# A four-layer graph network on one core: x of four groups ahead of the weights, a third group with x^T by TensorE, later constants, halved copies, the last norm by VectorE's statistics

## The chip, the cores and the metric

The kernel runs on one core of a Trainium2 chip. The metric is the device time of one execution in microseconds. Engine names in the profile: PE is TensorE (PEld its weight loads), DVE is VectorE, ACT is ScalarE, POOL is GpSimd, SP is SyncE, which here only issues transfers.

## The reference

x has 64 samples of 256 nodes with 128 features, adj is 256 x 256, all float32. Four layers follow one another, each with a residual and a norm over the features (here cut to the core):

```python
# layer 0: Chebyshev orders 1..3 of adj, twice the same adj: 7 weights
x = layernorm(x + sum_k(adj^k @ x @ W0[..., k]))
# layer 1
x = layernorm(x + adj @ (x @ w1) + b1)
# layer 2: A = adj + I, d = rowsum(A) ** -0.5
x = layernorm(x + (d A d) @ x @ w2.T + b2)
# layer 3: five steps of a gated graph cell, in_matrix = out_matrix = adj
def step(h):
    m = adj @ h;  av = concat([m, m])
    z = sigmoid(av @ w3.T + b3 + h @ u3.T + bu3)
    r = sigmoid(av @ w4.T + b4 + h @ u3.T + bu3)
    hv = tanh(av @ w5.T + b5 + (r * h) @ u5.T + bu5)
    return (1 - z) * h + z * hv
x = layernorm(x + step^5(x))
```

## The kernel before

The samples are taken in 32 groups of two; group g starts at sample 2g. A group's tiles are 128 partitions x 512. Every piece of work (a transfer, a few matmuls, an elementwise operation) is recorded as an operation with an engine, a cost, a lag, a rank, and the values that it reads and writes. A planner (`Plan.order`) then puts all operations in order: for each engine it takes the one that can start first by the recorded costs, among equals the one of lower place (rank plus a random part), in twelve tries of which it keeps the one that ends first by its own times. The order of each engine's instructions is thereby fixed before the kernel runs, and engines work through it strictly one after the other. An operation's cost and rank steer this order only. Up to twelve groups are under way at once, so the steady state mixes all layers.

Constants are recorded with `pre(rank, engine, cost, ...)`, `load` (by default on SP's queue) and `fetch`. They are:

- `a_nat`, the adjacency; `aT`, its transpose (TensorE `turn`, then a copy, L293); `a2T`, the transpose of its square (matmuls, then a copy, L303). The first product with x reads a2T. Short transposes of the identity (`warming`) stand between.
- `w0_raw` and from it `w0s`, `w0t` (layer 0's weights, centred over the features so that the norm needs no mean);
- `ahat`, `deg`, `dinv`, `anT` (layer 2's matrix: `degree` L354 to L358, a power on GpSimd L370, `rows` L362, a turn by TensorE, `columns` L366);
- for each matrix, five sums of its 128 x 128 blocks (`block_sums`, L383 to L387), names s_aT, s_a2T, s_anT, s_aTp;
- `wb` (w1, b1, b2, centred at L320, L321), and the gate weights: raw tiles, sums of their halves (`both`, L411, L413), and transposes of these by TensorE (w435u5T, w2u3T).

A group's product with a matrix (`propagate`) has a plain form, and a form of seven 128-column products (`seven`): GpSimd makes three differences of the input (tsq, tqq and the like, L744 to L751), TensorE does four products, then a fifth, then two more, and between them ACT and VectorE make sums from the bank in place (usq L770, wsq L773, mq L776, L780). The last two products overwrite a part of the bank that mq's sum reads, so they wait for it.

`record` opens a group: it loads x and forms x^T. A group that starts below `HEAD` is near: TensorE transposes x (`ptx`, L801), the product q with a2T is plain, and `inner` does layer 0 with plain products. Any other group is far: VectorE transposes 32 x 32 blocks of x (tx, L871), SP stores it to DRAM (dx, L874) and loads it back in another order in two transfers (xT, L879), q is by `seven`, and `inner_seven` forms four differences of xT and q on VectorE (sd, ss, se, sf, L635 to L644) and does layer 0 with fewer products. A transfer waits at the head of SP's queue for what it reads, and whatever stands behind it waits too.

The last layer's end has two forms. Six samples' worth of groups at the end (`END`) use `closing`: TensorE makes the centred sum s in a bank, `spread_of` has ACT square each 128 columns with a sum (L543: an activation and a readout for each), GpSimd raises the four sums to -1/2 (rs, L547), and VectorE multiplies (L704); then the output is stored (L939).

Of the kernel before, what the change touches and what calls it, by code (L numbers as in the profile page):

```python
# [11 lines left out]
OP = mybir.AluOpType  # L12
AX = mybir.AxisListType

P = 128
NB = 2
ACTIVE = 12
HEAD = 4
LEVEL = 7
PLAIN = 0  # L20
END = 6
# [3 lines left out]
EPS = 1e-5  # L25
# [147 lines left out]
def act_cost(elements):  # L173
    return elements / 1.2 + 165
# [3 lines left out]
def kernel(  # L178
# [30 lines left out]
    nc = tc.nc  # L209
    B, N, C = x.shape  # L210
    T = N // P
# [12 lines left out]
    plan = Plan(slots, G - LEVEL)  # L224
# [10 lines left out]
    def pre(rank, engine, cost, run, reads=(), writes=(), lag=None, joint=False, after=()):  # L235
        lag = lag or {"SP": 2300, "PE": 260, "DVE": 260, "ACT": 130, "POOL": 100}[engine]
        return plan.add(engine, cost, lag, rank, run, reads, writes, after, joint)
# [4 lines left out]
    def fetch(rank, o, src, v, queue, after=()):  # L242
        e, cost = QUEUES[queue]
        return pre(rank, queue, cost, lambda: e.dma_start(o, src), [], [v], lag=5000, joint=True, after=after)

    def load(rank, name, shape, src, keep=True, queue="SP", lag=2300):
        v = constant(name, shape) if keep else Val("w", shape, name)
        e, cost = QUEUES[queue]
        pre(rank, queue, cost, lambda: e.dma_start(v.ap, src), [], [v], lag=lag)
        return v  # L250
# [3 lines left out]
    half = const.tile([P, Q], F32, name="half")  # L254
# [20 lines left out]
    a_nat = load(-9, "a_nat", [P, T, N], adj.rearrange("(t p) m -> p t m", p=P), False)  # L275
    aT, a2T = constant("aT", [P, T, N]), constant("a2T", [P, T, N])
    p_at, p_a2, p_an = temp("p_at"), temp("p_a2"), temp("p_an")

    def turn(ps, src):
        for mt in range(T):  # L280
            for nt in range(T):
                nc.tensor.transpose(ps.ap[:, mt * N + nt * P:mt * N + (nt + 1) * P],
                                    src.ap[:, nt, mt * P:(mt + 1) * P], ident)

    def flat(v):
        return v.ap.rearrange("p t n -> p (t n)")

    def turned_early():
        turn(p_at, a_nat)
        warming(4)  # L290

    pre(-8, "PE", 8 * 110, turned_early, [a_nat], [p_at, warm])
    pre(-8, "ACT", act_cost(512), lambda: nc.scalar.copy(flat(aT), p_at.ap), [p_at], [aT])  # L293

    def square():
        for mt in range(T):
# [3 lines left out]
        warming(2)  # L300

    pre(-8, "PE", pe_cost(N, 4) + 220, square, [a_nat, aT], [p_a2, warm])
    pre(-8, "ACT", act_cost(512), lambda: nc.scalar.copy(flat(a2T), p_a2.ap), [p_a2], [a2T])  # L303


    w0_raw = load(-1, "w0_raw", [P, C, K0], w0, lag=7300)

    w0s = constant("w0s", [P, 4, C])
# [16 lines left out]
    centred = pre(-7, "DVE", 1600, lambda: centre(w0s, w0m), [w0s], [w0s, w0m])  # L325
# [15 lines left out]
    aTp = constant("aTp", [P, T, N])  # L341
# [8 lines left out]
    ahat, anT = Val("w", [P, T, N], "ahat"), constant("anT", [P, T, N])  # L350
    deg, dinv = constant("deg", [P, T]), constant("dinv", [P, T])
# [14 lines left out]
            nc.vector.tensor_scalar(anT.ap[:, mt, :], p_an.ap[:, mt * N:(mt + 1) * N], dinv.ap[:, mt:mt + 1],  # L366
                                    None, op0=OP.mult)

    pre(0.3, "DVE", 1500, degree, [a_nat], [ahat, deg])
    pre(0.3, "POOL", 700, lambda: nc.gpsimd.tensor_tensor(dinv.ap, deg.ap, half[:, :T], op=OP.pow), [deg], [dinv])  # L370
    pre(0.9, "DVE", 600, rows, [ahat, dinv, w0s], [ahat])
    pre(1.1, "PE", 4 * 110, lambda: turn(p_an, ahat), [ahat], [p_an])
    pre(0.3, "DVE", 900, columns, [p_an, dinv], [anT])


    sums_of = {}
# [1 line left out]
    def block_sums(rank, name, aTs, after=()):  # L378
        v = constant(f"s_{name}", [P, 5, P])
        a11, a12, a21, a22 = (aTs.ap[:, kt, t * P:(t + 1) * P] for t in range(T) for kt in range(T))  # L380

        def run():
            nc.vector.tensor_add(v.ap[:, 0, :], a21, a22)  # L383
            nc.vector.tensor_sub(v.ap[:, 1, :], v.ap[:, 0, :], a11)
            nc.vector.tensor_sub(v.ap[:, 2, :], a11, a21)
            nc.vector.tensor_sub(v.ap[:, 3, :], a12, v.ap[:, 1, :])
            nc.vector.tensor_scalar(v.ap[:, 4, :], a22, -1.0, None, op0=OP.mult)  # L387

        pre(rank, "DVE", 1200, run, [aTs], [v], after=after)
        sums_of[aTs] = v  # L390

    block_sums(0.6, "aT", aT)
    block_sums(0.6, "a2T", a2T)
    block_sums(0.6, "anT", anT, (centred,))
    block_sums(0.7, "aTp", aTp, (centred,))

    wb, wbm = constant("wb", [P, 3, C]), constant("wbm", [P, 3])

    made = pre(-7, "DVE", 100, lambda: nc.vector.tensor_copy(wb.ap[:, 1:3, 0], w0s.ap[:, :2, 0]), [w0s], [wb])
    fetch(0.6, wb.ap[:, 0, :], w1, wb, "SP")
    for i, b in ((1, b1), (2, b2)):
        last = fetch(0.5, wb.ap[:, i, :], bass.AP(tensor=b.tensor, offset=b.offset, ap=[[0, P], [1, C]]), wb, "POOL", (made,))
    pre(0.9, "DVE", 1100, lambda: centre(wb, wbm), [wb, w0s], [wb, wbm])
    w1c, b1c, b2c = ((wb, wb.ap[:, i, :]) for i in range(3))
    raw = {name: load(0.6, f"raw_{name}", [P, src.shape[1]], src, False, lag=9000)
           for name, src in (("w2", w2), ("w4", w4_w), ("w3", w3_w), ("w5", w5_w), ("u3", u3_w), ("u5", u5_w))}
    both = {name: Val("w", [P, C], f"both_{name}") for name in ("w4", "w3", "w5", "w34")}
    for name in ("w4", "w3", "w5"):  # L410
        pre(0.4, "DVE", 220, lambda o=both[name], i=raw[name]: nc.vector.tensor_add(  # L411
            o.ap, i.ap[:, :C], i.ap[:, C:]), [raw[name]], [both[name]])
    pre(0.4, "DVE", 220, lambda: nc.vector.tensor_sub(both["w34"].ap, both["w3"].ap, both["w4"].ap),  # L413
        [both["w3"], both["w4"]], [both["w34"]])

    less = constant("less", [P, P])
# [28 lines left out]
    def nat(v):  # L445
        return v.ap.rearrange("p (q c) -> p q c", c=C)
# [21 lines left out]
    class Group:  # L468
# [68 lines left out]
        def spread_of(self, tag, s):  # L537

            y, ve, rs = self.val("w", "y" + tag), self.val("ve", "ve" + tag), self.val("rs", "rs" + tag)

            def squares():
                for q in range(self.q):
                    nc.scalar.activation(nat(y)[:, q, :], nat(s)[:, q, :], AF.Square, scale=C ** -0.5,  # L543
                                         bias=root[:, 0:1], accum_out=ve.ap[:, q:q + 1])

            def scales():
                nc.gpsimd.tensor_tensor(rs.ap, ve.ap, half[:, :self.q], op=OP.pow)  # L547

            self.act(squares, [s], [y, ve], 390 * self.q)
            self.add("POOL", 1040, 100, scales, [ve], [rs])  # L550
            return y, rs

        def normalise_centred(self, tag, s):
# [133 lines left out]
        def closing(self, y, hT, e, behind):  # L687

            s, hc = self.val("bank", "s3"), self.val("w", "hc")
            way, out_ = self.by_tile  # L690
            self.act(lambda: nc.scalar.copy(out_(hc), way(hT)), [hT], [hc])

            def turned(v, start, stop):
                for q in range(self.q):
                    mm(s.ap[:, q * P:(q + 1) * P], v.ap[:, q * P:(q + 1) * P], less.ap, start and q == 0, stop, shared=True)

            def early():
                turned(hc, True, False)
                mm(s.ap, ident, y.ap, False, False, shared=True)

            self.pe(pe_cost(P, self.q) + pe_cost(self.width), early, [hc, y, less], [s], behind=(behind,))
            self.pe(pe_cost(P, self.q), lambda: turned(e, False, True), [e, less], [s])
            o, rs = self.spread_of("3", s)
            self.dve(lambda: nc.vector.tensor_tensor(nat(o), nat(s), rs.ap[:, :, None].to_broadcast([P, self.q, C]),  # L704
                                                     op=OP.mult), [s, rs], [o])
            return o
# [152 lines left out]

        def record(self):  # L860
            x_ = self.val("x", "x")
            plan.add("SP", 450, (6000, 9000)[self.start // NB] if self.start < HEAD else 2700, self.rank() - 1.5, lambda: nc.sync.dma_start(nat(x_), self.view(x)), [], [x_],
                     self.load_gate)

            near = self.start < HEAD
# [2 lines left out]
            else:  # L868

                turn, far, xT = self.val("w", "tx"), self.val("dram", "dx"), self.val("w", "xT")  # L870
# [13 lines left out]
            y = self.normalise_centred("0", s0)  # L884


            for tag, ats, w, bias in (("1", aT, w1c, b1c), ("2", anT, w2T, b2c)):
# [15 lines left out]
                y = self.normalise_centred(tag, self.added(tag, py, yb))  # L903
# [42 lines left out]
    for i, nb in enumerate(sizes):  # L946
        group = Group(sum(sizes[:i]), nb)
        end = group.start + nb
        done = [o for o in groups if o.start + o.nb <= end - NB * ACTIVE]
        loaded = [o for o in groups if o.start + o.nb <= end - NB * (ACTIVE + 2)]  # L950
        if done:
            group.gate = (done[-1].last,)
        if loaded:
            group.load_gate = (loaded[-1].last,)
        elif group.start >= HEAD:
            group.load_gate = (groups[i - 2].first,)
        group.record()
        groups.append(group)
# [4 lines left out]
    with tc.manual_schedule():  # L963
        for op in plan.order():
            for v in op.vals:
                if v.tile is None:
# [3 lines left out]
                    if v.shape != full:  # L970
                        n = 1
# [37 lines left out]
```

## Time and profile before

| | |
|---|---|
| median of 3 runs | 1342.21 us (1341.92 to 1343.14) |
| the profiled execution's own time | 1342.32 us |
| its span in the trace | 1340.5 us |
| mean granted TensorE clock | 0.997 |
| TensorE instructions (matmul passes) | 6915 |
| VectorE, ScalarE, GpSimd instructions | 2577, 2361, 998 |

A float32 matmul shows as two passes, each with its weight load, so the trace counts each product twice; a transpose is one pass. Busy shares are those of the span. Idle time in square brackets ahead of an instruction names what ended it. A line number is that of the kernel before; almost all matmuls are at L219, since one helper issues them, so they are told apart by their tiles (out<-weights,moving).

### The profile page before, as it was taken

The numbers are of one execution on the slowest core, as the hardware profiler recorded it, in microseconds if no ns is written. First come the engines' busy times: TensorE is split into PE (matmuls) and PEld (weight loads), VectorE is DVE, ScalarE is ACT, GpSimd is POOL, SyncE is SP. The second block draws the span as 40 slices with busy tenths as digits, with TensorE's granted clock in tenths as the row PEclk, the third lists the DMA queues.
The fourth block names the chain that finished last, engine by engine and source line by source line (L and its number), as shares of the span: only waits on it lengthen the run. The fifth ranks groups of instructions, "written<-read, shape, count | busy, mean of one in ns | idle before, by whom it ended". The sixth has DMA issues, their size and how long they took to land.

```text
span 1340.5 us, 22669 instructions
## 1 busy us (share of the span) xinstructions
PE 1325.7 (99%) x6915; PEld 931.9 (70%) x6915; DVE 1039.0 (78%) x2577; ACT 773.6 (58%) x2361; POOL 636.1 (47%) x998
## 2 busy tenths in 40 slices
PE   8999999999999999999999999999999999999997
PEld 7987666667877766777766686777676776566554
DVE  7867767897778778788888797778876778777776
ACT  4587464645666664656655565655556786444445
POOL 5788352325646543447453454545345574232212
PEclk9999999999999999999999999999999999999999
DMA  7412333433433342333442343424322233333323
GB/s 190 131 33 79 88 95 87 141 107 96 115 95 111 95 121 70 110 95 103 121 124 74 108 134 87 119 71 119 101 73 68 60 111 103 112 109 95 89 85 103
DMA packets 269305, 134.87 MB, mean 101 GB/s; under 512 B 175712, under 2 KB 240864, under 8 KB 269184
## 3 DMA queue, kind: packets, MB, share of 16 engines
q1 hardware_dynamic: 268928, 133.29, 34.6%
q8 instruction: 55, 0.90, 0.3%
q0 software_dynamic: 256, 0.13, 0.1%
q14 instruction: 66, 0.54, 0.1%
HBM read 67.31 MB, written 65.80 MB: 99 GB/s over the span
## 4 chain that ended last, share of the span: by engine, by line
PE 97%; DVE 1%; DMA 1%; issue 0%; SPq 0%; ACT 0%; POOLq 0%; POOL 0%; ACTq 0%
PE pr L219 31%; PE ph L219 21%; PE pmg L219 19%; PE py L219 11%; PE pm L219 8%; PE pz L219 4%; PE pmq L219 3%; DMA x<-in_x_dram 1%; PE s L219 1%; DVE tx L871 0%; SPq L345 0%; DVE sd L635 0%; ACT y L543 0%; POOLq L1004 0%; DVE both_w L411 0%
## 5 line engine op out<-in xcount | busy, mean ns | idle before, releaser
L219 PE MATMUL pr<-mg,w435u5T 128*128 128x512 f32 x640 | 319.7, 593 | 0.0
L744 POOL TENSOR_TENSOR tsg<-h 128x256 f32<-128x256 f32 x128 | 94.0, 735 | 281.1 <-DMA h<-dh 200.4
L850 ACT ACTIVATE r<-pr,bsum 128x512 f32<-128x512 f32 x160 | 105.2, 658 | 123.4 <-PE pr L219 114.9
L850 ACT ACTIVATE pr<-pr,bsum 128x512 f32<-128x512 f32 x160 | 105.2, 658 | 118.0 <-PE pr L219 117.7
L547 POOL TENSOR_TENSOR rs<-ve,half 128x4 f32<-128x4 f32 x99 | 101.6, 1027 | 145.8 <-ACT y L543 137.2
L543 ACT ACTIVATE y<-s,root 128x128 f32<-128x128 f32 x396 | 153.7, 392 | 28.2 <-DVE s L565 25.5
L857 DVE TENSOR_TENSOR d<-ph,hT 128x512 f32<-128x512 f32 x160 | 109.6, 685 | 72.1 <-ACT ph L850 69.2
L219 PE MATMUL ph<-mg,w435u5T 128*128 128x512 f32 x320 | 163.3, 593 | 0.0
L219 PE MATMUL ph<-rh,w435u5T 128*128 128x512 f32 x320 | 162.7, 593 | 0.0
L219 PE MATMUL pr<-hT,w2u3T 128*128 128x512 f32 x320 | 162.2, 593 | 0.0
L219 PEld LDWEIGHTS pr<-mg,w435u5T 128*128 128x128 f32 x640 | 108.8, 191 | 70.3 <-issue 57.6
L850 ACT ACTIVATE ph<-ph,bsum 128x512 f32<-128x512 f32 x160 | 105.4, 659 | 57.8 <-PE ph L219 55.5
L219 PEld LDWEIGHTS pmg<-aTp,h 128*128 128x128 f32 x512 | 90.5, 196 | 64.8 <-issue 40.5
L857 DVE TENSOR_TENSOR rh<-r,hT 128x512 f32<-128x512 f32 x160 | 109.3, 683 | 33.1 <-ACT r L850 29.5
L558 ACT ACTIVATE y<-s,rs 128x128 f32<-128x128 f32 x384 | 122.1, 394 | 5.2 <-POOL rs L547 4.8
L857 DVE TENSOR_TENSOR pr<-pr,d 128x512 f32<-128x512 f32 x157 | 108.1, 691 | 1.7 <-ACT pr L850 0.5
L857 DVE TENSOR_TENSOR hT<-hT,pr 128x512 f32<-128x512 f32 x157 | 106.1, 678 | 1.3
L219 PE MATMUL pmg<-s_aTp,tsg 128*128 128x128 f32 x768 | 106.7, 275 | 0.0
L219 PEld LDWEIGHTS ph<-rh,w435u5T 128*128 128x128 f32 x320 | 58.5, 190 | 62.7 <-issue 46.2
L219 PE MATMUL pmg<-aTp,h 128*128 128x128 f32 x512 | 98.1, 279 | 0.0
L891 POOL TENSOR_TENSOR yb<-y,wb 128x512 f32<-128x512 f32 x64 | 81.7, 1277 | 34.3 <-ACT y L558 33.0
L780 DVE TENSOR_TENSOR mg<-pmg,usg 128x256 f32<-128x256 f32 x160 | 66.6, 418 | 39.7 <-PE pmg L219 38.3
(200 smaller groups left out, 2826.4 us busy)
## 6 DMA issues: line engine op xcount, KB each, us to landing
dh<-th SPq DMA_DIRECT2D x160, 256.0 KB, 2.0
h<-dh SPq DMA_DIRECT2D x256, 128.0 KB, 2.5
x<-in_x_dram SPq DMA_DIRECT2D x32, 256.0 KB, 3.2
hT<-dh SPq DMA_DIRECT2D x128, 64.0 KB, 2.1
out_dram<-y SPq DMA_DIRECT2D x32, 256.0 KB, 2.5
dx<-tx SPq DMA_DIRECT2D x30, 256.0 KB, 2.5
xT<-dx SPq DMA_DIRECT2D x60, 128.0 KB, 2.7
dn<-tn SPq DMA_DIRECT2D x29, 256.0 KB, 2.0
```

The source lines that it names most:

```text
L219: nc.tensor.matmul(o, lhsT, rhs, start=start, stop=stop, skip_group_check=shared)
L543: nc.scalar.activation(nat(y)[:, q, :], nat(s)[:, q, :], AF.Square, scale=C ** -0.5, bias=root[:, 0:1], accum_out=ve.ap[:, q:q + 1])
L547: nc.gpsimd.tensor_tensor(rs.ap, ve.ap, half[:, :self.q], op=OP.pow)
L558: nc.scalar.mul(nat(y)[:, q, :], nat(s)[:, q, :], rs.ap[:, q:q + 1])
L744: nc.gpsimd.tensor_tensor(ts.ap[:, :2 * P].rearrange("p (x c) -> p x c", x=2), ins(h)[:, 1], ins(h)[:, :, 0], op=OP.subtract)
L780: nc.vector.tensor_tensor(o(m, slice(1, 3)), o(ps, slice(1, 3), False), both, op=OP.add)
L850: self.act(lambda: nc.scalar.activation(t.ap, ps.ap, func, bias=bias[1], scale=1.0), [ps, bias[0]], [t], act_cost(self.width) + 100)
L857: self.dve(lambda: nc.vector.tensor_tensor(out(t), way(a), way(b), op=op), [a, b], [t])
L891: nc.gpsimd.tensor_tensor(nat(yb), nat(y), bias[1][:, None, :].to_broadcast([P, self.q, C]), op=OP.add)
```

## The change

- `HEAD` goes from 4 to 6, so three groups instead of two are near: group 2 (samples 4 and 5) has x^T by TensorE, the plain q and `inner`.
- The x loads of groups 0 to 3 have no gate on an earlier group, and larger planned lags; those of groups 2 and 3 were gated by the first operation of groups 0 and 1.
- The copies of aT and a2T are made in two halves, the first on ACT and the second on VectorE.
- Layer 2's matrix, block sums of anT and aTp, w1's load, the gate weights' loads and their sums get later ranks; `degree` waits for w0s.
- The last group's norm takes its variance from VectorE's statistics (`spread_at_once`) instead of ACT's squares.

```diff
-HEAD = 4
+HEAD = 6
...
-    pre(-8, "ACT", act_cost(512), lambda: nc.scalar.copy(flat(aT), p_at.ap), [p_at], [aT])
+    def halved(v, ps):
+
+        pre(-8, "ACT", act_cost(N), lambda: nc.scalar.copy(v.ap[:, 0, :], ps.ap[:, :N]), [ps], [v], joint=True)
+        pre(-8, "DVE", 420, lambda: nc.vector.tensor_copy(v.ap[:, 1, :], ps.ap[:, N:]), [ps], [v], joint=True)
+
+    halved(aT, p_at)
...
-    pre(-8, "ACT", act_cost(512), lambda: nc.scalar.copy(flat(a2T), p_a2.ap), [p_a2], [a2T])
+    halved(a2T, p_a2)
...
-    pre(0.3, "DVE", 1500, degree, [a_nat], [ahat, deg])
-    pre(0.3, "POOL", 700, lambda: nc.gpsimd.tensor_tensor(dinv.ap, deg.ap, half[:, :T], op=OP.pow), [deg], [dinv])
-    pre(0.9, "DVE", 600, rows, [ahat, dinv, w0s], [ahat])
-    pre(1.1, "PE", 4 * 110, lambda: turn(p_an, ahat), [ahat], [p_an])
-    pre(0.3, "DVE", 900, columns, [p_an, dinv], [anT])
+    pre(2.3, "DVE", 1700, degree, [a_nat, w0s], [ahat, deg])
+    pre(2.3, "POOL", 720, lambda: nc.gpsimd.tensor_tensor(dinv.ap, deg.ap, half[:, :T], op=OP.pow), [deg], [dinv])
+    pre(2.3, "DVE", 800, rows, [ahat, dinv], [ahat])
+    pre(2.3, "PE", 4 * 110, lambda: turn(p_an, ahat), [ahat], [p_an])
+    pre(2.3, "DVE", 900, columns, [p_an, dinv], [anT])
...
-    block_sums(0.6, "anT", anT, (centred,))
-    block_sums(0.7, "aTp", aTp, (centred,))
+    block_sums(2.4, "anT", anT, (centred,))
+    block_sums(2.6, "aTp", aTp, (centred,))
...
-    fetch(0.6, wb.ap[:, 0, :], w1, wb, "SP")
+    fetch(1.9, wb.ap[:, 0, :], w1, wb, "SP")
...
-    raw = {name: load(0.6, f"raw_{name}", [P, src.shape[1]], src, False, lag=9000)
+    raw = {name: load(2.0, f"raw_{name}", [P, src.shape[1]], src, False, lag=9000)
...
-        pre(0.4, "DVE", 220, lambda o=both[name], i=raw[name]: nc.vector.tensor_add(
+        pre(2.0, "DVE", 300, lambda o=both[name], i=raw[name]: nc.vector.tensor_add(
...
-    pre(0.4, "DVE", 220, lambda: nc.vector.tensor_sub(both["w34"].ap, both["w3"].ap, both["w4"].ap),
+    pre(2.0, "DVE", 300, lambda: nc.vector.tensor_sub(both["w34"].ap, both["w3"].ap, both["w4"].ap),
...
+        def spread_at_once(self, tag, s):
+
+            st, mv, ve, rs, y = (self.val(k, n + tag) for k, n in (
+                ("st", "st"), ("mv", "mv"), ("ve", "ve"), ("rs", "rs"), ("w", "y")))
+
+            def stats():
+                for q in range(self.q):
+                    nc.vector.bn_stats(st.ap[:, q * 6:(q + 1) * 6], nat(s)[:, q, :])
+                for q in range(self.q):
+                    nc.vector.bn_aggr(mv.ap[:, 2 * q:2 * q + 2], st.ap[:, q * 6:(q + 1) * 6])
+                nc.vector.tensor_scalar(ve.ap, mv.ap.rearrange("p (q k) -> p k q", k=2)[:, 1], EPS, None, op0=OP.add)
+
+            self.dve(stats, [s], [st, mv, ve], 260 * self.q + 110)
+            self.add("POOL", 1040, 100, lambda: nc.gpsimd.tensor_tensor(rs.ap, ve.ap, half[:, :self.q], op=OP.pow),
+                     [ve], [rs])
+            return y, rs
...
-            o, rs = self.spread_of("3", s)
+            o, rs = (self.spread_at_once if self.start >= B - NB else self.spread_of)("3", s)
...
-            plan.add("SP", 450, (6000, 9000)[self.start // NB] if self.start < HEAD else 2700, self.rank() - 1.5, lambda: nc.sync.dma_start(nat(x_), self.view(x)), [], [x_],
+            plan.add("SP", 450, dict(zip(range(0, 4 * NB, NB), (6000, 9000, 10500, 9000))).get(self.start, 2700), self.rank() - 1.5, lambda: nc.sync.dma_start(nat(x_), self.view(x)), [], [x_],
...
-        elif group.start >= HEAD:
+        elif group.start >= 4 * NB:
             group.load_gate = (groups[i - 2].first,)
```

More of the change, by code (lines that the diff above doesn't have):

```diff
@@ L283, in turn @@
                                     src.ap[:, nt, mt * P:(mt + 1) * P], ident)
-    def flat(v):
-        return v.ap.rearrange("p t n -> p (t n)")
     def turned_early():
```

## The prediction

> **What bounds the kernel now.** I read the page from the top, then the waits of TensorE, then stretches of time, then single instructions.
>
> ```profile
> PE 1325.7 (99%) x6915; PEld 931.9 (70%) x6915; DVE 1039.0 (78%) x2577; ACT 773.6 (58%) x2361; POOL 636.1 (47%) x998
> PE 97%; DVE 1%; DMA 1%; issue 0%; SPq 0%; ACT 0%; POOLq 0%; POOL 0%; ACTq 0%
> ```
>
> Busy shares first, then the chain that ended last: TensorE is 99% busy and 97% of the chain. So only three things can move the time: TensorE's work, the few places where it isn't fed, and the stretches before its first and after its last matmul. The table of its waits gives the places:
>
> ```profile
> PE pmq L219 <- DVE mq L776: 5.1, 1, 5.1
> PE warm L270 <- POOL ident masks.py:199: 1.4, 1, 1.4
> PE pz L219 <- DVE u L664: 1.0, 1, 1.0
> PE pm L219 <- ACT us L786: 0.4, 1, 0.4
> ```
>
> Four waits in 1340 us, and all in the first 42. The stretches of time (columns: stretch; busy us of PE, weight loads, DVE, ACT, POOL with counts; granted clock; DMA share; GB/s) and VectorE's timeline show what the large one is:
>
> ```profile
> 28.00:33.00 5.00, 0.00 (x0) 0.00 (x0) 4.70 (x12) 0.68 (x4) 3.24 (x5) 0.81 0.95 270
> 33.00:38.30 5.30, 4.88 (x22) 4.58 (x23) 3.57 (x12) 1.66 (x7) 0.00 (x0) 0.54 0.78 207
> 42.00:48.00 6.00, 6.00 (x52) 5.97 (x53) 5.36 (x15) 2.55 (x12) 3.90 (x7) 1.00 0.01 3
> ```
>
> ```profile
> 26.11 1.13 DVE L871 STREAM_TRANSPOSE tx<-x 128x512 f32<-128x512 f32 x1 [1.79 <-DMA x<-in_x_dram]
> 27.17 0.82 DVE L366 TENSOR_SCALAR anT<-p_an,dinv 128x256 f32<-128x256 f32 x2
> 28.27 1.08 DVE L871 STREAM_TRANSPOSE tx<-x 128x512 f32<-128x512 f32 x1 [0.28 <-DMA x<-in_x_dram]
> ...
> 32.74 0.28 DVE L776 TENSOR_TENSOR mq<-wsq,pmq 128x128 f32<-128x128 f32 x1
> ```
>
> TensorE stops at 27.95 and starts at 33.07, because the small sum mq (L776) stands in VectorE's queue behind transposes of x tiles that landed late, the two anT columns and five anT sums. Then TensorE runs at half clock until 38.3 (22 matmuls in 5.3 us, against 52 in 6 us later). Loss: 5.12 + half of the 4.88 us busy at half clock + 0.35 + 1.01 for the two later waits = **8.9 us**. A count agrees: the matmuls that stand between 9.09 (first product of x) and 48.53 are 30.0 us at the steps seen in undisturbed stretches (0.2165 us for a pass of 256 columns, 0.1115 for one of 128), and took 39.44: 9.4. I use 9.1.
>
> **What the Trainium skill says.** "TensorE: Matmul & The Clock Gate", Part 1, "What's actually happening": the clock is halved after an idle, free-running window of about 3.4 us. The trace agrees: 5.12 us idle, half clock from about 31.5. So a remaining wait under 3.4 us costs only itself. "DMA: Bandwidth & Descriptors", "Anatomy of one DMA": about 2.0 us fixed for a DMA (stated for another issue path). SP's first dx here was issued at 14.91 and its reader followed at 17.03, 2.1; under load x takes 3.1 to 5.5. "SBUF — State Buffer", "Who interferes with whom": VectorE's tensor_tensor with two SBUF inputs contends with GpSimd's reads. Here the s_aTp sums took 0.50 to 0.81 beside GpSimd's tsq, against 0.28 alone.
>
> **The change part by part.**
>
> 1. *Copies halved.* aT and a2T were ACT copies of 512 columns, 0.59 each. Now ACT (256 columns: 0.37) and DVE (0.41, row of mg L780) work together, at most 0.41, so 0.18 less each. Of the first, about half is lost, as the square that follows runs partly at the cold clock (8 passes in 2.54, full speed would be 1.73), whose end I take as fixed in time. TensorE's first product of x starts at about 8.8 instead of 9.09. VectorE is free for its halves since the degree (0.43 + 0.49 + 0.69) has left this place. Gain **0.3**; bounds 0 to 0.4.
>
> 2. *Group 2 (samples 4, 5) by the near path.* Its q by plain product, its inner part plain, x^T by TensorE. In the planned order 42 passes of 128 columns go (42 x 0.1115 = 4.68), 24 passes of 256 come (5.20), and 4 transposes (0.45). Cost **1.0** on the bound; nothing hides it. It also takes one tx (1.1), a dx and two xT transfers off VectorE and SP.
>
> 3. *x of groups 1 to 3 before the weights.* (x0, x1 and so on are the tiles of groups 0, 1 ...) On SP the order is now a_nat, x0, w0_raw, x1, x2, x3, then the weights, aTp, the last w3; 8 issues of about 0.48, so x3 is issued at 3.3. Before, 1.7 MB had landed by about 8.3, so x2 and x3 land by 8 to 9, where x2 and x3 were issued at 10.4 and 11. The weights come 1 to 2 us later and are read from 15 on (w3, the last, issued at about 11, from 19): hidden by 4 us; a weight later than that would hold VectorE's queue, as the changed sums stand in it before tx of x4. GpSimd's bias transfers are issued at 13.8 to 24 as its queue allows, and are read at 22 (b1, b2) and 33: hidden too.
>
> 4. *Constants later.* VectorE's queue now, from w0s ready at 12.5: tx of x3 to 13.6; wb, w0t, both w4 to 15.1; degree to 16.7; both w5; s_aTp (1.1 alone, 2.7 beside GpSimd; I take 2.0) to 19.0; both w3, rows, w34 to 20.4; tx of x4 to 21.5; sd, centring wb to 22.9. There it **waits for x5**: SP issues x5 only behind the store of x4's transpose, at 22.0, and with 3.6 it lands at 25.6. Then tx to 26.7; columns to 27.5; sd waits for its xT to 28.4; s_anT to 30.0; usq; x6 (SP: behind the next dx, 27.15) at 30.8; tx to 31.9; wsq; tx of x7 to 33.2; and mq, the sum that TensorE waited for before, at about **33.5**.
>
> TensorE's queue from 8.8, full: both groups' q and inner, group 2's q and x^T (to 25.3), the constants' transposes (to 26.5), four products of x3's q (27.4), group 2's inner (31.1), group 0's first propagate and x4's q (32.8). There stands the last part of x3's q, which needs mq. So group 2's q, transposes and first products, 5.6 us, now stand ahead of the reader of mq. Left: 33.5 - 32.8 = 0.7. I take 0.7, and 0.6 for small waits at the next two such sums, where VectorE is only 0.5 us ahead: **1.3** in all; bounds 0 and 3.4, up to which the clock holds.
>
> 5. *Last norm.* Now the last group's four squares with readouts run on ACT behind the group before, to 1335.6:
>
> ```profile
> 1335.37 0.24 ACT L543 ACTIVATION_READ_ACCUMULATOR y<-s,root 128x1 f32 x1
> 1335.69 1.01 POOL L547 TENSOR_TENSOR rs<-ve,half 128x4 f32<-128x4 f32 x1 [0.39 <-ACT y L543]
> ```
>
> Statistics on VectorE (0.87 + 0.36 + 0.17, rows of an earlier group's) would start at 1333.6 and end at 1335.0. But GpSimd holds the group before's power from 1334.29 to 1335.30, so the last power starts at 1335.3, not 1335.0. Gain **0.4**; bounds 0.2 and 0.6.
>
> Sum: -9.1 - 0.3 + 1.0 + 1.3 - 0.4 = -7.5, from the profiled execution's 1342.32, which is 0.1 above the median of the runs: **1334.8**.
>
> **The rivals.**
>
> *The same stall again.* If x loads need 5.5 (the longest seen) and not 3.6, x5 lands at 27.5, x6 3.7 us later than above, mq at about 37.2. TensorE then waits 4.4, the clock halves, 2.5 more: 1333.5 + 6.9 = 1340.4. For it: SP still puts each x behind a dx that waits for VectorE, so delays add. Against: the DMA share fell from 0.95 in the old stall to an easier schedule, since two x loads and a transpose's transfers have gone from it.
>
> *Slower: SP's chain x, tx, dx, next x becomes the pace.* One link is 1.1 + 0.4 + 3.6 = 5.1; at 7.0 (x in 5.5) four links lose 7.6, in two waits over 3.4 us each, so the clock halves twice (2 x 2.5): 1333.5 + 12.6 = 1346. It decides from a link of about 6.6. Against: at 5.5 for every load there would have to be a crowd on the queues, and the crowd was at 28 to 38.
>
> *No wait left.* mq a little earlier: 1333.2.
>
> *The middle reordered.* The planner's random tries give a new order; a wait of 3 us there gives 1338. The old order had none after 42 us, with VectorE at 78%.
>
> **How the numbers follow.** Forecast and its small waits 0.68 (1333.2 to 1337), no wait 0.06, reordered middle 0.08, same stall 0.12 (a part below 1339.5), slower chain 0.06. A measurement here can tell about 0.2%, 2.7 us, from no change. Faster: 0.68 + 0.06 + 0.06 + 0.04 = 0.84; same: 0.02 + 0.08 = 0.10; slower 0.06. The range reaches from no wait, 1333.0, to most of the same stall, 1339.5.
>
> **What would show it.** TensorE's waits: nothing near 5 us on mq, a wait of about 0.7 near 33, clock 1.00 from 9 us on. VectorE waits 2 to 3 us for x near 23. py of group 2 in passes of 256 columns. Last power on GpSimd right behind the one before. Wrong if a wait on mq exceeds 3.4 us with a clock of 0.5 after it, or if TensorE waits after 60 us.

## The result, and the profile after

| | before | after |
|---|---|---|
| median of 5 runs on the same chip | 1342.21 us (1341.62 to 1343.14) | **1335.56 us** (1335.40 to 1336.13) |
| ratio | | **0.9951**, 95% interval 0.9937 to 0.9964 |
| profiled execution, and its span | 1342.32, 1340.5 | 1335.75, 1334.0 |
| mean granted TensorE clock | 0.997 | 0.999 |

The change takes 6.65 us off the median; 1334.8 was forecast. The page's busy line and the shares of its chain hardly move, as the change touches only some 7 us of a TensorE that was 99% busy already:

```profile
PE 1324.2 (99%) x6901; PEld 930.1 (70%) x6901; DVE 1041.9 (78%) x2574; ACT 770.5 (58%) x2355; POOL 633.0 (47%) x995
PE 97%; DVE 1%; issue 0%; ACT 0%; POOL 0%; POOLq 0%; ACTq 0%
```

TensorE's waits (engine, tile and line that waited; who released it; us in total, times, longest) show what is gone. The wait of 5.1 us on mq has left the table, and the largest that remains, apart from the first instructions' wait for the identity, is on w0s:

```profile
PE warm L270 <- POOL ident masks.py:199: 1.4, 1, 1.4
PE py L219 <- DVE w0s L323: 1.0, 1, 1.0
PE pmq L219 <- DVE mq L795: 0.3, 1, 0.3
```

The stretches of time around the old stall (stretch; busy us of PE, weight loads, DVE, ACT, POOL with counts; granted clock; DMA share; GB/s) show TensorE busy throughout and its clock whole:

```profile
28.00:33.00 5.00, 5.00 (x32) 4.59 (x32) 4.39 (x12) 3.45 (x15) 3.96 (x8) 1.00 0.78 214
33.00:38.00 5.00, 5.00 (x36) 4.41 (x36) 4.79 (x14) 2.06 (x8) 5.00 (x9) 1.00 0.95 258
```

In VectorE's timeline (start, duration, instruction, idle before it) the transposes of late x tiles are still there, with mq behind them, at 33.61 where the prediction had 33.5:

```profile
21.00 1.12 DVE L890 STREAM_TRANSPOSE tx<-x 128x512 f32<-128x512 f32 x1
...
26.02 1.16 DVE L890 STREAM_TRANSPOSE tx<-x 128x512 f32<-128x512 f32 x1 [2.54 <-DMA x<-in_x_dram]
...
30.98 1.10 DVE L890 STREAM_TRANSPOSE tx<-x 128x512 f32<-128x512 f32 x1 [0.17 <-DMA x<-in_x_dram]
...
32.56 1.11 DVE L890 STREAM_TRANSPOSE tx<-x 128x512 f32<-128x512 f32 x1 [0.31 <-DMA x<-in_x_dram]
33.61 0.24 DVE L795 TENSOR_TENSOR mq<-wsq,pmq 128x128 f32<-128x128 f32 x1
```

So mq is no earlier than it was (32.74 before). TensorE comes to its reader later: at 33.99, with no idle time listed ahead of it (by the starts of the matmuls before it, it could have started 0.16 earlier, so mq and TensorE arrive almost together). That is the first hint at which part of the change did the work. TensorE's timeline:

```profile
13.67 0.67 PE L219 MATMUL py<-w0s,xT 128*128 128x256 f32 x2 [0.99 <-DVE w0s L323]
...
33.99 0.46 PE L219 MATMUL pmq<-s_a2T,x 128*128 128x128 f32 x2
```

One of the two pieces that make it later is the new wait for w0s, which the prediction did not have. GpSimd's timeline and VectorE's at that place:

```profile
10.23 0.73 POOL L763 TENSOR_TENSOR tsq<-x 128x256 f32<-128x256 f32 x1 [8.92 <-DMA x<-in_x_dram]
```

```profile
10.01 0.38 DVE L313 TENSOR_TENSOR w0s<-w_raw,ident 128x128 f32<-128x128 f32 x1
10.31 1.77 DVE L315 TENSOR_TENSOR w0s<-w_raw 128x128 f32<-128x128 f32 x3
```

The three sums that centre w0s took 1.77 us for 0.98 before, beside GpSimd's first difference (tsq) of an x tile. That is group 3's x now, which has landed by 10.2; before, GpSimd's first tsq stood at 13.81, long behind the sums. Both instructions read two SBUF inputs.

### The profile page after: what moved, and what is told of

Same layout as the page of the kernel before. It is cut to its first block, busy times and chain, and to the rows that moved or that the text cites. A ratio compares the mean times of both kernels' runs of the same rounds, so it can differ in the third digit from the quotient of the medians.

```text
span 1334.0 us, 22643 instructions
## 1 busy us (share of the span) xinstructions
PE 1324.2 (99%) x6901; PEld 930.1 (70%) x6901; DVE 1041.9 (78%) x2574; ACT 770.5 (58%) x2355; POOL 633.0 (47%) x995
## 4 chain that ended last, share of the span: by engine, by line
PE 97%; DVE 1%; issue 0%; ACT 0%; POOL 0%; POOLq 0%; ACTq 0%
PE pr L219 30%; PE ph L219 20%; PE pmg L219 19%; PE py L219 12%; PE pm L219 7%; PE pz L219 4%; PE pmq L219 3%; PE s L219 1%; PE warm L270 0%; PE p_a L219 0%; DVE rh L876 0%; DVE w0s L315 0%; DVE ss L657 0%; ACT y L545 0%; DVE se L660 0%
## 5 line engine op out<-in xcount | busy, mean ns | idle before, releaser
L219 PEld LDWEIGHTS pmg<-s_aTp,tsg 128*128 128x128 f32 x768 | 95.8, 192 | 0.0
```

The source lines that it names most:

```text
L219: nc.tensor.matmul(o, lhsT, rhs, start=start, stop=stop, skip_group_check=shared)
```

## The experiments

Seven versions have parts of the change or leave one out, one has a fourth near group, two move a single operation near w0s (told of below, not in the table), and the best one and the changed kernel were run once more side by side. Times are medians of 5 runs, of 21 for constants alone and loads alone; the kernel before had medians of 1342.26 to 1342.73 beside them. Most intervals of the ratios overlap, so that differences under about 2 us between versions are read from the traces and not from the medians.

| version | parts of the change in it | us | ratio to before, 95% interval |
|---|---|---|---|
| constants alone | late ranks | 1340.93 | 0.9987 (0.9980 to 0.9993) |
| loads alone | the rule for x loads | 1343.66 | 1.0011 (1.0004 to 1.0017) |
| **near alone** | third near group | **1335.33** | 0.9954 (0.9942 to 0.9967) |
| loads and near | both | 1335.31 | 0.9953 (0.9941 to 0.9966) |
| two near | all but the third near group | 1337.84 | 0.9964 (0.9952 to 0.9977) |
| no tail | all but the last norm | 1335.05 | 0.9948 (0.9936 to 0.9961) |
| near and tail | third near group, last norm | 1334.44, 1334.59 | 0.9942 (0.9928 to 0.9955), 0.9946 (0.9933 to 0.9958) |
| four near | a third and a fourth near group | 1337.05 | 0.9958 (0.9946 to 0.9971) |
| changed, again | all | 1335.24 | 0.9946 (0.9932 to 0.9959) |

### Constants alone

The kernel before with the change's ranks of layer 2's matrix, the block sums of anT and aTp, w1 and the gate weights:

```diff
-    pre(0.3, "DVE", 1500, degree, [a_nat], [ahat, deg])
+    pre(2.3, "DVE", 1700, degree, [a_nat, w0s], [ahat, deg])
...
```

> The kernel before with only the constants' later ranks (layer 2's matrix, the sums of anT and aTp, w1, the gate weights); two near groups, whole copies, ACT's squares. Theory A (the gain needs both: fewer constants ahead of mq on VectorE, and group 2's plain work ahead of its reader on TensorE): VectorE reaches mq at about 30.6 instead of 32.7, TensorE waits 2.5 to 3 us, the clock holds; about 1337.5. Rival B (the order of the constants on VectorE is all of it): the wait on mq is under 1 us; about 1335. Rival C (the constants were covered, x's landing sets mq): a wait of 5 us and half clock as before; 1342.

Measured 1340.93, a gain of 1.8 by the medians of that chip (1342.69 before). The two profiled executions differ by 1.5: 1.1 is an earlier start (first product of x at 7.99, before at 9.09), and 0.6 is shorter waits. The stall did not go: it fell into two. TensorE's timeline, and its stretches there:

```profile
29.06 0.49 PE L219 MATMUL pmq<-a2T,x 128*128 128x128 f32 x2 [2.44 <-ACT usq L786]
31.41 0.80 PE L219 MATMUL pmq<-s_a2T,x 128*128 128x128 f32 x2 [1.87 <-DVE mq L776]
```

```profile
31.00:32.00 1.00, 0.59 (x2) 0.59 (x3) 1.00 (x3) 0.00 (x0) 1.00 (x2) 0.70 0.95 297
32.00:33.00 1.00, 1.00 (x6) 1.00 (x6) 0.97 (x3) 0.00 (x0) 0.79 (x2) 0.50 0.67 175
33.00:34.00 1.00, 1.00 (x7) 1.00 (x6) 1.00 (x6) 0.27 (x1) 0.00 (x0) 0.50 1.05 355
34.00:35.00 1.00, 0.77 (x4) 0.47 (x3) 1.00 (x6) 0.19 (x1) 0.00 (x0) 0.59 1.05 310
```

Neither wait reaches 3.4 us, and still the clock is halved from about 31.4 to 34.8 (the third column from the right: 0.70 in the first stretch and 0.59 in the last place the two ends). The 0.49 us of work between the waits did not keep the clock up. So step 4's ranks alone are not the cause, and the prediction's sentence that a wait under 3.4 us costs only itself does not hold. Its reading of the kernel before was off too: a mean clock of 0.81 from 28 to 33 puts the halving at 31.1 and not at 31.5, which is 3.1 us after TensorE stopped at 27.95.

### Loads alone, near alone, and both

Loads alone is the kernel before with this; near alone is the kernel before with `HEAD = 6` and 4 in the place of `HEAD` in these two lines; the third has all of it. In both versions with this load rule the weights keep their old ranks, and the last of the four x is still not early: it is issued at 11.52 in loads alone (11.03 before) and at 9.13 in the third, against 3.32 in the changed kernel. So they test the edit, and not step 3's early x of group 3.

```diff
-(6000, 9000)[self.start // NB] if self.start < HEAD else 2700
+dict(zip(range(0, 4 * NB, NB), (6000, 9000, 10500, 9000))).get(self.start, 2700)
-        elif group.start >= HEAD:
+        elif group.start >= 4 * NB:
```

> The kernel before with the new rule for x loads alone (x of group 2 ahead of the weights, group 3 among them): group 2 keeps the far path, constants, copies and last norm are old. Theory A (the stall was VectorE's queue behind late x tiles, and needs both earlier x and more TensorE work ahead of mq's reader): the stall shrinks but does not go, waits of 1 to 3 us in all before 45 us, clock mostly full, 1336 to 1339. Theory L (the loads are the whole of it): 1334.5 to 1335.5. Theory N (the near path is the whole of it): 1341 to 1342.3.

> The kernel before with three groups on the near path alone; the x loads keep their place behind the weights, constants, copies and last norm are old. The near path costs 1.0 of TensorE's time. Theory A: a tx, a dx and two xT transfers go from VectorE and SP, and 5.6 us more of TensorE's work stands ahead of mq's reader, but x of groups 2 and 3 still lands at 14 to 17; waits of 1 to 4 us, 1336 to 1340. Theory N: 1335 to 1336. Theory L: no gain, 1342 to 1343.5.

> The kernel before with only the early ungated loads of x for groups 0 to 3 and the third near group. Theory A: TensorE has 5.6 us more to do before it needs mq, so the wait is 0 to 1 us even with the old ranks of the constants; about 1335.8. Rival B (constants are all of it): mq is as late as before or later, a wait of 3 to 5 us; about 1340 to 1343. Without the halved copies the first product of x starts at 9.09 as before in both.

Loads alone: 1343.66, nothing gained and by the interval a little lost. All three theories missed it, N by the least; A missed as the stall stayed (TensorE's timeline of this version):

```profile
29.93 0.46 PE L219 MATMUL pmq<-s_a2T,x 128*128 128x128 f32 x2 [1.12 <-ACT y L543]
35.54 0.77 PE L219 MATMUL pmq<-s_a2T,x 128*128 128x128 f32 x2 [3.77 <-DVE mq L776]
```

Near alone: **1335.33, the whole gain**, as theory N has it; A had expected waits of 1 to 4 us, and behind the first product of x there is one of 0.7 and one of 0.2. Its waits of TensorE, and VectorE's timeline:

```profile
PE warm L270 <- POOL ident masks.py:199: 1.4, 1, 1.4
PE py L219 <- DVE v L664: 0.7, 1, 0.7
PE pm L219 <- DVE m L776: 0.2, 1, 0.2
PE p_a L219 <- ACT aT L293: 0.2, 1, 0.2
```

```profile
22.85 1.15 DVE L871 STREAM_TRANSPOSE tx<-x 128x512 f32<-128x512 f32 x1 [2.04 <-DMA x<-in_x_dram]
...
30.92 1.12 DVE L871 STREAM_TRANSPOSE tx<-x 128x512 f32<-128x512 f32 x1
31.96 0.24 DVE L776 TENSOR_TENSOR mq<-wsq,pmq 128x128 f32<-128x128 f32 x1
```

x of groups 2 and 3 still lands late here (issued at 10.49, as before), VectorE still waits 2 us for an x, and mq comes at 31.96, only 0.8 earlier than before. But TensorE comes to mq's reader later, without a wait. The reader in this version, and in the kernel before:

```profile
32.70 0.39 PE L219 MATMUL pmq<-s_a2T,x 128*128 128x128 f32 x2
```

```profile
33.07 0.80 PE L219 MATMUL pmq<-s_a2T,x 128*128 128x128 f32 x2 [5.12 <-DVE mq L776]
```

32.70 is 24.31 us behind this version's first product of x (8.39), against 27.95 - 9.09 = 18.86 before: it has 5.45 us more to do first. Step 2 had put 5.6 us of group 2's plain products ahead of that reader, and the passes in the trace are these: 24 more of 256 columns (q, and layer 0's py) and 4 more transposes of x, while what else comes and goes, 10 passes of 128 columns each, balances.

With the load rule added to it, 1335.31: by the median it brings nothing more. But single executions of the versions with the near path and the old ranks of the constants are 2 to 3 us longer: one of five here (1338.43), two of five with the load rule (1337.14 and 1337.90), one of ten of near and tail (1337.44). Of the twenty executions of the versions with three near groups, the early loads and the later constants (changed, changed again, no tail, and the one below with block sums moved) none is above 1336.13. The profile of loads and near is that of 1337.14, and there a later mq is waited for (1.1 us at 41.84). Whether the other parts guard against such executions is not shown.

### All but the third near group

```diff
-HEAD = 6
+HEAD = 4
```

> The changed kernel with two near groups instead of three (loads of x still early, constants later, copies halved, last norm by VectorE). Theory A: 1.0 us of TensorE's work less, but the work that stood ahead of the first far reader has gone, so waits of 2 to 4 us come back near 28 to 40; 1336 to 1338. Rival B: no wait comes back, and the kernel gains the 1.0; 1334.6.

Measured 1337.84: a gain of 4.8 without the third near group (0.4 of it from the last norm, see below), with no wait over 1.4 us. Loads and constants, of which one alone loses 1.3 and the other gains 1.8, do remove the stall together (the halved copies are in this version too, but are worth 0.2, see below); with the weights ranked later, all four x are issued by 3.4. So these parts together and the near path alone are two ways to remove the same stall. Here it is mq that moves: the first one stands at 24.70 in VectorE's timeline, against 32.74 before.

```profile
24.70 0.28 DVE L795 TENSOR_TENSOR mq<-wsq,pmq 128x128 f32<-128x128 f32 x1
```

This version saves step 2's 1.0 us of products, and loses some 3 us more than the changed kernel in small waits. TensorE's timeline:

```profile
13.87 0.67 PE L219 MATMUL py<-w0s,xT 128*128 128x256 f32 x2 [1.39 <-DVE w0s L323]
...
25.12 0.46 PE L219 MATMUL pmq<-s_a2T,x 128*128 128x128 f32 x2 [0.49 <-ACT v L619]
...
61.26 0.46 PE L219 MATMUL pm<-s_anT,y 128*128 128x128 f32 x2 [0.63 <-DVE m L795]
```

### The wait for w0s, from both sides

GpSimd's first difference of group 3's x kept back by a dependency on the copy `made` from w0s, which lets the planner order everything anew:

```diff
-            self.add("POOL", 830, 100, ts01, [h], [ts])
+            self.add("POOL", 830, 100, ts01, [h], [ts], behind=(made,) if tag == "q" and self.start == 6 else ())
```

> The changed kernel with GpSimd's differences of group 3's x placed behind its transfers of b1 and b2, which wait for VectorE's w0s. Theory D (the wait of 1.0 for w0s in the changed kernel is VectorE held up by GpSimd's reads): VectorE's three sums of w0_raw take 1.0 instead of 1.77, TensorE waits under 0.3 for w0s; 1334.8. Rival (w0s is late because w0_raw, a2T or the queue ahead of it is late): the wait stays at 1.0 and the time at 1335.5.

The sums took 1.00 and not 1.77, and the wait fell from 0.99 to 0.21; so far the contention theory is right. But the time was 1339.44, ratio 0.9976 (0.9967 to 0.9985): the planner's new order put in waits of 1.0, 0.8, 0.8 and 0.7 elsewhere. This is the prediction's rival of the reordered middle, met in a version whose edit touches one small operation. Therefore the next version moves one operation in the finished order and leaves the rest in place: `moved`, the block sums of a2T, goes behind `centred`, the operation that makes w0s ready.

```diff
-        for op in plan.order():
+        ops = plan.order()
+        ops.remove(moved)
+        ops.insert(ops.index(centred) + 1, moved)
+        for op in ops:
```

> The changed kernel with one step moved in the order it ends with: VectorE's five sums of a2T stand behind the centring of w0s instead of ahead of its sums. Everything else keeps its place. Theory D (the 0.99 us wait for w0s comes from VectorE: its queue reaches the w0 sums at 10.0, after w0_raw has long landed, and they run beside GpSimd's tsq from 10.23 on): the sums start at about 9.0, take 1.0 and not 1.77, w0s is ready at about 12 and TensorE does not wait for it; VectorE is about 0.7 ahead from there, the wait on mq stays below 0.6; time about 1334.8, 0.8 below the changed kernel. Rival (the w0s wait only hides a later one, the wait on mq or x landing): the wait for w0s goes, but mq stays at 33.6 and its wait grows to 1.2; time 1335.5 as before. Rival 2 (w0_raw itself lands late): the sums start no earlier than 10.

Measured 1334.94, ratio 0.9946 (0.9933 to 0.9960). The sums start at 8.00, TensorE has no wait for w0s, and the first rival is right all the same: the wait moved. VectorE's and TensorE's timelines of this version:

```profile
8.30 0.98 DVE L315 TENSOR_TENSOR w0s<-w_raw 128x128 f32<-128x128 f32 x3
...
30.86 1.12 DVE L890 STREAM_TRANSPOSE tx<-x 128x512 f32<-128x512 f32 x1 [2.10 <-DMA x<-in_x_dram]
...
33.07 0.25 DVE L795 TENSOR_TENSOR mq<-wsq,pmq 128x128 f32<-128x128 f32 x1
```

```profile
33.46 0.46 PE L219 MATMUL pmq<-s_a2T,x 128*128 128x128 f32 x2 [1.51 <-DVE bsum L443]
```

The reader waits 1.5 us (named after bsum, which stands just behind mq; by the times it is mq that released it: the reader starts 0.14 behind mq's end, as in the changed kernel), because mq hangs on an x tile that lands at 30.86 and not on VectorE's speed. In the changed kernel the wait for w0s takes the place of this one. That the time comes near theory D's 1334.8 is no success of theory D. The profiled execution took 1335.46, 0.29 less than that of the changed kernel: its first product of x stood at 7.71, 0.8 earlier, and its waits cost 0.5 more. What made the median 0.5 lower still is not shown.

### The last norm

```diff
-            o, rs = (self.spread_at_once if self.start >= B - NB else self.spread_of)("3", s)
+            o, rs = self.spread_of("3", s)
```

> The changed kernel with the last group's norm by ScalarE's squares again; the order of all else is the same. Step 5 of the prediction (0.4 at the end): 1336.0. Theory S (the stores take it back: the last two stores of 256 KB stand closer together and the gain is lost between the last issue and the end): the last y starts about 0.4 later behind TensorE's end, but the stretch from TensorE's end to the end of the span stays at 6.9 to 7.0, time 1335.5 to 1335.7.

The median was 1335.05, below the changed kernel's 1335.56, so both numbers of the expectation missed. The order of all else is the same, and the two profiled executions (1335.05 and 1335.75) show where the time came from: the start. TensorE's first product of x stood at 8.06 here and at 8.53 there, and this time it was GpSimd that lost the clash (tsq 1.42, the sums 0.98), so that the wait for w0s was 0.4 and not 1.0. Together that is 1.0, of which the old norm takes 0.4 back at the end. GpSimd's timeline at the end, of this version and of the changed kernel:

```profile
1326.75 1.01 POOL L549 TENSOR_TENSOR rs<-ve,half 128x4 f32<-128x4 f32 x1 [3.51 <-ACT y L545]
1328.14 1.01 POOL L549 TENSOR_TENSOR rs<-ve,half 128x4 f32<-128x4 f32 x1 [0.39 <-ACT y L545]
```

```profile
1327.82 1.01 POOL L549 TENSOR_TENSOR rs<-ve,half 128x4 f32<-128x4 f32 x1 [3.50 <-ACT y L545]
1328.79 1.01 POOL L568 TENSOR_TENSOR rs<-ve,half 128x4 f32<-128x4 f32 x1
```

With squares the last power stands 1.39 behind the one before, with statistics 0.97, right behind it: 0.42 saved. All of it reaches the last store: from the start of TensorE's last matmul to the issue of that store it is 4.15 to 4.17 us in all seven profiles with squares and 3.73 to 3.74 in all seven with statistics. So theory S, by which the stores take it back, is wrong. What the store then takes to the end of the span varies, 3.07 to 3.57 us over the fourteen profiles, and the kernel before had the shortest. From the issue of the third-last store to the end of the span, the seven with squares have 8.03, 8.13, 8.14, 8.33, 8.34, 8.34 and 8.52, mean 8.26; the seven with statistics have 7.74, 7.93, 7.94, 7.94, 7.94, 7.94 and 7.95, mean 7.91. The gain is **0.35**. The pair of the first comparison alone (8.03 and 7.94) would have said 0.1.

### Near path and last norm only, and a fourth near group

The first is near alone with the tail's two edits; the second is near alone with `HEAD = 8`.

> Three groups on the near path and the last norm by VectorE's statistics, nothing else of the change: x loads, constants and copies as before. TensorE's order is that of the run with three near groups alone (1335.33), which waits 0.9 us in all. Theory N (the near path is the gain and the last norm adds step 5's 0.3 to 0.4): 1335.0, no wait on mq near 33, last y 3.8 after the issue of the store before the last two, not 4.2. Rival (the last norm gives nothing): 1335.3 and more. If the loads, constants and halves bring anything of their own, it is slower than the changed kernel's 1335.56.

> The kernel before with four groups on the near path (samples 0 to 7) and nothing else of the change. Doubles step 2's cost where there is little left to hide: theory N with step 2's working (42 passes of 128 columns go, 24 of 256 and 4 transposes come, 1.0 us on the bound for each group): 1336.3, TensorE's busy time before 60 us 1.0 above that of three near groups. Rival (fewer tx on VectorE still pays): 1335.0 or less. Rival 2 (x of group 3 is not there when TensorE wants it, new wait of 1 to 2): 1337.5 to 1338.5.

Near and tail: 1334.44, the lowest of all. It has near alone's waits (0.7 on v, 0.2 on m) and ends sooner: the last y stands 3.81 behind the issue of the store before the last two, 4.23 in near alone. Four near: 1337.05, 1.7 above near alone, where 0.3 less, 1.0 more or 2.2 to 3.2 more stood open; none of the three numbers (the two ratios do not part the versions). The spans of the two profiles differ by 1.83, and by the starts of the matmuls that falls into 0.9 for the products, as step 2 has it, 0.7 of waits (1.1 idle in one wait of ph on rh, at 892) and 0.2 in the last store. With the stall gone, this near group brought nothing and cost its products.

> The near path and the last norm alone, a second time, beside the changed kernel on the same chip. If the x loads, late constants and halved copies cost a little (the wait for w0s of 0.4 to 1.0 and the small wait on mq, which this version has not): 0.5 to 1.1 below the changed kernel. If its 1334.44 was a lucky start: within 0.3 of it.

> The changed kernel a second time, on the same chip as the version with the near path and the last norm alone: 1335.0 to 1335.8; the wait for w0s 0.3 to 1.1, as x of group 3 lands just before, in or after VectorE's w0 sums.

Side by side on one chip: 1334.59 and 1335.24, the latter with a wait for w0s of 0.9, within its expected range. The medians differ by 0.65; the two ratios, 0.9946 each, do not part them. So by these the smaller version does as well with two of the five parts. That it is faster than the changed kernel is not shown.

## Why the prediction was right, and where it was not

The forecast of 1334.8 was 0.8 below the median, and the steps can be checked one by one on the two profiled executions, which differ by 6.57. Lost time is read from the starts of successive matmuls, against their steps in undisturbed stretches:

| step | forecast | measured |
|---|---|---|
| old losses between first product and 48 us gone, new ones come (steps 3, 4) | -9.1 + 1.3 = -7.8 | 9.44 lost before, 1.67 after: -7.8 |
| first product earlier (step 1) | -0.3 | -0.57, of which 0.2 by the copies |
| third near group (step 2) | +1.0 | +0.96 by the count of passes; 0.9 for the fourth |
| last norm (step 5) | -0.4 | -0.1 in this pair; -0.35 over fourteen profiles |
| later waits | 0 | +0.9 |

The measured terms add up to -6.6. The later waits are small pauses of the new order: 0.5 at 572.9 on mq (0.34 of it listed as idle) and 0.2 to 0.3 each at 370.4 and 781.3 on rh and at 1085.5 on us, against 0.45 of such pauses before. The prediction had put this term at nothing, and had named a wait of TensorE after 60 us as a sign of being wrong: by its letter the sign came, with 0.3 us in the table of waits.

**The bound and the mechanism** were right: the stall was VectorE's small sum behind transposes of late x, and it goes when TensorE has other work ahead of the sum's reader. Near alone shows this directly.

**Step 3's early loads and step 4's late constants were credited with a share that they don't have beside the near path.** The walk in step 4 is right as a walk of this kernel (mq 33.5, measured 33.61), but it was never made without them. The runs show mq at 31.96 without either. The 5.6 us of step 2's products, which stand as one clause at the end of step 4, are enough by themselves. Loads alone and constants alone do not undo the stall; both together do it without the near path.

**Step 3 had x3 landing at 8 to 9, and step 4 had w0s ready at 12.5.** x3's reader started at 10.2, and w0s was ready for TensorE at 13.67. The prediction quoted from the Trainium skill, "SBUF — State Buffer", section "Who interferes with whom", that VectorE's tensor_tensor with two SBUF inputs contends with GpSimd's reads, and priced it for the s_aTp sums; it did not look at which sums the earlier x would now meet. Three profiles of the same order show three outcomes. In the changed kernel VectorE lost (sums 1.77, tsq 0.73), in no tail GpSimd lost (tsq 1.42, sums 0.98), and in changed, again, VectorE lost 0.2 in the sums (1.20) and 0.5 in the last block sum of a2T ahead of them (0.75 for 0.22). The page says that issue order decides who blocks. Where GpSimd began ahead of VectorE's slowed instructions (10.23 and 10.31 in the first case, 9.90 and 10.07 in the third) VectorE was the slow one, and where it began inside the sums (10.00, sums from 9.84) it was the slow one itself, which agrees.

**Step 4's wait of 0.7 on mq** shrank to 0.16, because TensorE came 1.0 later through w0s; with w0s early it is 1.5. That the sum of small waits, 1.3, came out in size (1.67, of which 1.15 at w0s) is luck: it came in another place and for another reason.

**Step 1** forecast 0.3; 0.2 of it can be shown, and for another reason. ACT and VectorE do not work together: VectorE's half of each copy starts when ACT's half has ended (a2T: ACT from 8.07 for 0.37, VectorE from 8.48), and the profile names ACT's half as what it waited for. VectorE's timeline of the changed kernel:

```profile
8.48 0.42 DVE L293 COPY a2T<-p_a 128x256 f32<-128x256 f32 x1 [1.38 <-ACT a2T L292]
```

Why it waits is not shown. What is saved is that TensorE's first product of x starts at 8.53, when ACT's half alone is there: from the last pass of the square to that product it is 0.87 us in all six profiles with halves and 1.05 to 1.06 in all eight with whole copies, 0.18 less. At aT the same saving is hidden in most profiles behind TensorE's own short transposes (0.03). In the starting times themselves none of it can be seen: six profiles with halves have the first product at 7.71 to 8.76, mean 8.41, and eight with whole copies at 7.99 to 9.15, mean 8.44. The clock's rise is what sets them: by the granted clock it comes at 4.1 to 7.3, and the 8 passes of the square took 1.89 to 2.75. The Trainium skill, "TensorE: Matmul & The Clock Gate", Part 1, "What's actually happening", calls the window free-running and the start run-variable, and these runs agree.

**Of the rivals**, the reordered middle (0.08) came in a neighbour of this kernel (1339.44), so it was rightly kept in the range. The same stall, the slower chain on SP and the version without any wait did not come.

## What to carry to other kernels

A small operation that the bound engine waits for can be cured from the reader's side: put independent work ahead of its reader, and leave the late queue as it is. When several parts of a change aim at one stall, work out each of them alone before summing; here one part of five was enough against the stall, and two others together were a substitute for it. After moving a load earlier, look at what its first reader now runs beside.

## What the runs showed of the hardware that was not expected

- Two waits of TensorE of 2.44 and 1.87 us with 0.49 us of work between them halved the clock for about 3.4 us (constants alone). In the kernel before it was halved 3.1 us into the wait of 5.12, and in loads alone 2.8 us into the wait of 3.77 (a mean clock of 0.80 from 34 to 35, TensorE's last matmul ending at 31.77).
- The three 128x128 sums of w0s took 0.98, 1.20 or 1.77 us in the same order of instructions, by the moments at which one transfer landed and VectorE came to the sums (no tail, changed again, changed).
- The last 256 KB store took 3.07 to 3.57 us from its issue to the end of the span over fourteen profiles, where the stretch ahead of it, from TensorE's last matmul to that issue, repeated within 0.02 for each form of the norm. So 0.4 us at the end is not read from one pair of spans.
